# Batch 1's row flags in a graph-attention kernel: from sums on ScalarE, stored and read back, in place of GpSimd's sums and a matmul

## Chip, cores and metric

The kernel runs on one core of a Trainium2 chip. The metric is the device time of one execution in microseconds; lower is better. Times before are the median of three runs; the profile shows one execution.

## The reference

For each of 16 batches there are 512 nodes with 512 features (x), one condition vector (cond), and an integer mask with 11 labels for each pair of nodes. The part that matters here is the row flag: a node whose features sum to zero gets no condition.

```python
row_zero = exp_v.sum(-1) == 0
q_exp = jnp.where(row_zero[..., None], 0.0, q[:, None, :])
vcq = jnp.concatenate([exp_v, q_exp], axis=-1)
self_feat = vcq @ W_self.T + b_self
output = self_feat
for d in range(2):
    # A: the mask (d = 0) or its transpose, first 20 neighbours
    output = output + _gat_attention(self_feat, cond, vb, Wq[d], bq[d], Wk[d], bk[d], Wout[d], bout[d])
return exp_v + jax.nn.relu(output)
```

The attention has 16 heads and attends from every node to the first 20 nodes of its batch. Scores are self_feat times keys plus mask and label bias; their softmax weighs the 20 values.

## The kernel before

Everything is float32, and features lie on the partitions. The order of the instructions on each engine is the order in which the program issues them (a manual schedule, no scheduler); tiles of one tag share a few slots, and an instruction waits until its slot is free.

**Setup.** The keys of all batches are multiplied with the query weights ahead of time, so that a score needs one product with self_feat. The work comes in 22 "key bursts", `keys` (line 541), n = 0 to 21 in the loop at line 600. A burst has 12 to 16 small matmuls (ps_g, line 550) into two pairs of PSUM banks, which ScalarE (line 565) and VectorE (line 567) evict, half each, into a stage tile `st` (tag st, four slots). There are 16 stages, (0,0) to (3,3), four bursts to three stages or nearly so. When a stage is full, SP stores it with three transfers: batch 0's part into `g0` in SBUF (line 570), batch 1's into `g1_d` (line 573) and the others' into `g_d` (line 574, 1120 KB).

The pool of the banks has two slots, so a burst's matmuls wait for the evictions of the burst before. To fill that time a list `other` of side steps (lines 581 to 585) is handed out from burst 4 on (line 610): biases, row flags of batch 0, bias scores, a quarter of a self_feat block, a piece of the values (`values`, line 515), row flags of batch 1, and another self_feat block. Side steps are TensorE work but for the first. The last piece of each value tile is followed by a VectorE copy (line 531) and a store that GpSimd issues (line 533). v00, v01, v10, v11, v20 are those tiles; they share two slots of tag full with the score biases of `full_add`.

Beside the bursts, at fixed n, stand the mask's steps of batch 0: `mask_count` at 6 and 13, `mask_mul` at 7 and 15 (a ScalarE cast, line 210, and a GpSimd product), `mask_add` at 9 with `load_cq(0)`, `full_add` at 18.

**Row flags.** There are two ways in the kernel. For batches 0 and 1, `row_sums` (line 163) adds the four feature blocks of the transposed x with three GpSimd additions, and `row_flags` (line 170) sums over the partitions by a matmul with ones, so that every partition of `nzs[b]` has all 512 flags after a VectorE comparison (line 174). For batches 2 to 15, `load_xn` loads x again with nodes on the partitions, in two halves of 512 KB; `row_sum` (line 148) is a ScalarE ACTIVATE with a running sum, four a batch; `row_mask` (line 154) compares on VectorE and stores 2 KB into `nz_d`; `load_nz` (line 159) reads them back, broadcast to all partitions (256 KB). The flags are read by `self_copy` (line 202), which evicts self_feat.

**Batch loop.** Each of four node tiles (nt) of a batch has 16 score matmuls (ps_s, line 249) and some self_feat matmuls of this or the next batch (ps_sf, line 189); at nt = 2 the values of the batch before are applied (ps_o, line 314). VectorE, ScalarE and GpSimd do the softmax. Batch 1's flags are first read at b = 0, nt = 3. At b = 0, nt = 1, SP issues the loads of batch 1's mask and cq, six stores that clear `bd_d` (`clear_blocks`) and twelve copies that fill it (`blocks`); `load_values` at nt = 2 reads it.

Of the kernel before, what the change touches and what calls it, by code (L numbers as in the profile page):

```python
# [18 lines left out]
def gat_kernel(  # L19
# [24 lines left out]
    C = F // P  # L44
# [45 lines left out]
    def load_xn(b, h):  # L90
        t = xns[b, h] = load.tile([P, 2, F], F32, tag="xn", name=f"xn{b}_{h}")
        nc.sync.dma_start(t, xn[b].rearrange("(p j) f -> p j f", j=4)[:, 2 * h : 2 * h + 2])
# [70 lines left out]
    def row_sums(b):  # L163

        t = rss[b] = load.tile([P, 2, F], F32, tag="xn", name=f"rx{b}")[:, 0]
        nc.gpsimd.tensor_add(t, xs[b][:, 0], xs[b][:, 1])
        for k in range(2, C):
            nc.gpsimd.tensor_add(t, t, xs[b][:, k])
# [176 lines left out]
    with tc.tile_pool(name="setup", bufs=1) as sp:  # L345
# [151 lines left out]
        with tc.tile_pool(name="setup_g", bufs=4) as sg:  # L497
# [83 lines left out]
            other = [(biases, ()), (row_flags, (0,)), (bias_scores, (0,)), (bias_scores, (1,))]  # L581
            other += [(self_step, (0, 0, 0, i, k)) for i in range(2) for k in (0, 2)]
            other += [(values, (t, (d,), k)) for t in range(2) for d in range(2) for k in range(C)]
            other += [(values, (2, (0, 1), k)) for k in range(C)] + [(row_flags, (1,))]
            other += [(self_step, (0, 1, 0, i, k)) for i in range(2) for k in (0, 2)]

            halves = [(fc, hg, d, i) for fc in range(C) for hg in range(C) for d in range(2) for i in range(2)]
# [12 lines left out]
            for n, runs in enumerate(bursts):  # L600
                for i in range(len(rest)):
                    if i < (3 if n == 0 else 1) or any(fc == 0 and (d, hg) == rest[0] for fc, hg, d, _, _ in runs):
                        key_rows(*rest.pop(0))
                keys(runs)
                if rest:
                    for d in range(2):
                        bias_terms(d, n)
                    continue
                first = n if first is None else first
                while done * (len(bursts) - first) < (n + 1 - first) * len(other):  # L610
                    f, args = other[done]
                    f(*args)
                    done += 1
                if n == 6:
                    mask_count(0, 0)
                if n == 7:
                    mask_mul(0, 0)
                if n == 9:
                    mask_add(0, 0)
                    load_cq(0)  # L620
                if n == 11:
                    row_sums(1)
                if n == 13:
                    mask_count(0, 1)
                if n == 15:
                    mask_mul(0, 1)
                if n == 18:
                    full_add(0, 0)

    soft = ctx.enter_context(tc.tile_pool(name="soft", bufs=2))  # L630
    gp = ctx.enter_context(tc.tile_pool(name="gp", bufs=2))
# [3 lines left out]
    with tc.manual_schedule():  # L635
        load_keys(1)

        prev = None
        o = None
        banks = None  # L640
        for b in range(B):
            def ahead(nt):


                if nt < 2:
                    return ((b, nt, 1),)
                return ((b + 1, 0, 0), (b + 1, 1, 0)) if nt == 3 and b + 1 < B else ()

            for nt in range(NT):
                store()  # L650
                if nt == 1:
                    if b + 1 < B:
                        load_adj(b + 1, 0)
                        load_cq(b + 1)
                    if b == 0:
                        clear_blocks(zero)
                        blocks()
                if nt == 2:
                    load_values(b)
                    if b + 1 in rss and b > 0:  # L660
                        load_nz(b + 1)
                    if 0 < b < B - 1:
                        load_keys(b + 1)
                    if b + 2 < B:
                        load_x(b + 2)
                    if b + 1 < B:
                        load_adj(b + 1, 1)
                    if b + 2 < B:
                        load_xn(b + 2, 0)
                        load_xn(b + 2, 1)  # L670

                if prev is not None:
                    normal(*prev)
                ps = ps_s.tile([P, 2, 512], F32, tag="s", name=f"ps_s{b}_{nt}")
                for part in ahead(nt):
                    self_feat(*part)
                if nt == 2 and b > 0:
                    banks = [ps_acc.tile([P, 512], F32, tag="acc", name=f"ps_o{b - 1}_{q}") for q in range(4)]
                    for n in range(2):
                        attend(b - 1, n, [t[:, bass.ts(n, N // 2)] for t in banks])  # L680
                    o = work.tile([P, C, N], F32, tag="o", name=f"o{b - 1}")
                    finish(b - 1, o, (0, 1), banks)
                for g in range(2):
                    scores(b, nt, g, ps)

                if nt == 0 and b > 0:
                    mask_mul(b, 1)
                    mask_count(b, 1)
                if nt == 1:
                    mask_add(b, 1)  # L690
                if nt == 2 and b + 1 < B:
                    mask_mul(b + 1, 0)
                    mask_count(b + 1, 0)
                if nt == 3 and b + 1 < B:
                    mask_add(b + 1, 0)
                last = b == B - 1
                for part in ahead(nt):
                    self_copy(*part)
                if last and nt == NT - 1:
                    s = soft.tile(full, F32, tag="s", name=f"s{b}_{nt}", bufs=3)  # L700
                    weigh_half(b, nt, ps, s, 0)
                    turn(*prev)
                    weigh_half(b, nt, ps, s, 1)
                else:
                    s = weigh(b, nt, ps)
                    expo(s)
                    if prev is not None:
                        turn(*prev)
                if nt < NT - 1:
                    full_add(b, nt + 1)  # L710
                elif b + 1 < B:
                    full_add(b + 1, 0)
                if nt >= 2 and b > 0:
                    residual(b - 1, 2 * nt - 4, o)
                    residual(b - 1, 2 * nt - 3, o)
                if 0 < b < B - 1 and nt < 2:
                    row_sum(b + 1, 2 * nt)
                    row_sum(b + 1, 2 * nt + 1)
                    if nt == 1:
                        row_mask(b + 1)  # L720
                prev = (b, nt, s)
        store()
        b = B - 1
        turn_half(*prev, 0)
        turn_half(*prev, 1)

        o = work.tile([P, C, N], F32, tag="o", name=f"o{b}")
        out_b = out[b].rearrange("(c p) n -> p c n", p=P)
        most = [ps_acc.tile([P, 512], F32, tag="acc", name=f"ps_o{b}_{q}") for q in range(4)]
        pairs = [ps_s.tile([P, 2, 512], F32, tag="s", name=f"ps_o{b}_{q}_2") for q in range(2)]  # L730
        rest = [pairs[q // 2][:, q % 2] for q in range(4)]
        parts = []
        for lo, hi, banks in ((0, NT - 1, most), (NT - 1, NT, rest)):
            width = (hi - lo) * R
            parts.append((slice(2 * lo, 2 * hi), slice(lo * P, hi * P), width, banks))
            for n in range(2):
                attend(b, n, [t[:, bass.ts(n, width)] for t in banks], slice(lo, hi))
        for ts, ns, width, banks in parts:
            for q in range(4):
                c = bass.ds(q // 2 * 2, 2)  # L740

                def of(t):
                    return t[:, c].rearrange("p c (t q n) -> p c t q n", q=2, n=32)[:, :, ts, q % 2]

                nc.vector.tensor_add(  # L745
                    of(o), banks[q][:, : 2 * width].rearrange("p (c t n) -> p c t n", c=2, n=32), of(sfs[b])
                )
            for c in range(C):
                nc.scalar.activation(o[:, c, ns], o[:, c, ns], AF.Relu, bias=bo[:, c : c + 1])  # L749
        ns = parts[0][1]  # L750
        for c in range(3):
            nc.gpsimd.tensor_add(o[:, c, ns], o[:, c, ns], xs[b][:, c, ns])
            nc.sync.dma_start(out_b[:, c, ns], o[:, c, ns])
        ns = parts[1][1]
        nc.vector.tensor_add(o[:, :, ns], o[:, :, ns], xs[b][:, :, ns])
        nc.sync.dma_start(out_b[:, :, ns], o[:, :, ns])
        ns = parts[0][1]
        nc.vector.tensor_add(o[:, 3, ns], o[:, 3, ns], xs[b][:, 3, ns])
        nc.sync.dma_start(out_b[:, 3, ns], o[:, 3, ns])
# [46 lines left out]
```

## Time and profile before

| | us |
|---|---|
| median of 3 runs | 634.22 (633.94 to 636.79) |
| the profiled execution | 634.41 |
| its span, first to last instruction | 632.6 |
| TensorE busy | 618.7 (98%) |
| VectorE busy | 508.4 (80%) |
| GpSimd busy | 337.4 (53%) |
| ScalarE busy | 218.1 (34%) |

The granted TensorE clock is 0.994 of full speed over the span. The chain of work that ended last is followed back from the last instruction: at each step to what released it, or to the instruction before it on its engine. In timelines a row gives start, length, engine, line, operation, tile written and tiles read; a square bracket gives the idle time before it and what ended it. Matmul rows overlap, since they are pipelined. PEld is the loading of weights, which runs beside PE.

### The profile page before, as it was taken

How to read it: one execution, taken by the hardware profiler on the slowest of the kernel's cores; microseconds unless marked ns; L12 is line 12 of the kernel's file. 1: busy time of each engine (PE TensorE's matmuls, PEld its weight loads, DVE VectorE, ACT ScalarE, POOL GpSimd, SP SyncE). 2: the span in 40 equal slices, each digit the busy share in tenths (PEclk: the TensorE clock that was granted, in tenths of full speed). 3: DMA queues.
4: the chain of work that ended last, by engine and by line, in shares of the span. 5: the costliest groups of instructions: out<-in, count | busy, mean ns of one | idle time of the engine just before them, and what ended most of it. 6: DMA issues, size and time to landing. Idle time of an engine off the chain costs nothing.

```text
span 632.6 us, 16385 instructions
## 1 busy us (share of the span) xinstructions
PE 618.7 (98%) x6814; PEld 383.6 (61%) x6814; DVE 508.4 (80%) x815; ACT 218.1 (34%) x480; POOL 337.4 (53%) x258
## 2 busy tenths in 40 slices
PE   8999999999999999999999999999999999999993
PEld 6655459986565656565655656565656565656542
DVE  0566546879888888888888889797988888888886
ACT  1445321233342424242424233343334242424232
POOL 2405331446556464738392938474655646473853
PEclk9999999999999999999999999999999999999997
DMA  8999998628384565738392909292838465663322
GB/s 287 397 382 321 392 371 249 216 88 268 134 237 165 150 253 127 275 90 313 70 333 42 358 19 339 52 292 107 262 141 248 154 207 196 147 256 102 129 68 101
DMA packets 89569, 131.86 MB, mean 208 GB/s; under 512 B 8888, under 2 KB 59608, under 8 KB 87448
## 3 DMA queue, kind: packets, MB, share of 16 engines
q1 hardware_dynamic: 88824, 129.47, 61.7%
q0 software_dynamic: 672, 1.36, 0.8%
q8 instruction: 53, 0.87, 0.6%
q14 instruction: 20, 0.16, 0.1%
HBM read 90.89 MB, written 39.92 MB: 207 GB/s over the span
## 4 chain that ended last, share of the span: by engine, by line
PE 85%; DVE 2%; ACT 1%; issue 0%; DVEq 0%; ACTq 0%
PE ps_s L249 43%; PE ps_sf L189 33%; PE ps_o L314 6%; PE ps_v L523 1%; ACT o L749 0%; PE ps_nz L172 0%; DVE s L287 0%; DVE mx L278 0%; DVE o L745 0%; DVE s L279 0%; PE ps_g(3, 3, 0, 0, 2)0_778 L550 0%; PE ps_g(3, 2, 0, 1, 2)0_752 L550 0%; PE ps_g(3, 1, 1, 0, 2)0_724 L550 0%; PE ps_g(3, 0, 1, 1, 2)0_701 L550 0%; DVE ps_s L276 0%
## 5 line engine op out<-in xcount | busy, mean ns | idle before, releaser
L249 PE MATMUL ps_s<-g,sf 128*64 128x320 f32 x2048 | 287.6, 433 | 0.0
L249 PEld LDWEIGHTS ps_s<-g,sf 128*64 128x64 f32 x2048 | 155.4, 137 | 116.3 <-issue 6.2
L189 PE MATMUL ps_sf<-x,ws_v 128*64 128x256 f32 (+1 forms) x2048 | 222.0, 371 | 0.0
L189 PEld LDWEIGHTS ps_sf<-x,ws_v 128*64 128x64 f32 x2048 | 151.1, 137 | 67.5 <-issue 1.7
L296 POOL TENSOR_TENSOR s<-s,sm 128x640 f32<-128x640 f32 x63 | 80.1, 1271 | 145.5 <-DVE sm L295 134.8
L269 ACT ACTIVATE s<-s 128x640 f32<-128x640 f32 x63 | 46.5, 738 | 220.9 <-DVE s L264 220.9
L239 POOL TENSOR_TENSOR full<-cq,both 128x640 f32<-128x640 f32 x64 | 99.0, 1547 | 27.6 <-ACT both L230 23.5
L211 POOL TENSOR_TENSOR prod<-prod,wb_sb 128x880 f32<-128x880 f32 x32 | 61.3, 1915 | 56.5 <-ACT prod L210 56.5
L260 DVE TENSOR_TENSOR ps_s<-ps_s,full 128x640 f32<-128x640 f32 x63 | 52.3, 831 | 39.4 <-PE ps_s L249 39.4
L336 POOL TENSOR_TENSOR o<-o,x 128x512 f32<-128x512 f32 x60 | 75.5, 1281 | 0.0
L230 ACT COPY both<-add 64x80 f32<-64x80 f32 x128 | 32.8, 256 | 77.4 <-DVE add L225 76.3
L202 DVE SCALAR_TENSOR_TENSOR sf<-nz,qw,ps_sf 128x236 f32<-128x236 f32 (+1 forms) x128 | 52.6, 458 | 3.5 <-PE ps_sf L189 3.5
L333 ACT ACTIVATE o<-o,bo 128x512 f32<-128x512 f32 x60 | 40.0, 714 | 44.3 <-DVE o L327 44.3
L294 DVE TENSOR_REDUCE sm<-s 128x32 f32<-128x640 f32 x63 | 51.6, 818 | 4.4 <-ACT s L269 0.9
L262 DVE TENSOR_REDUCE mx<-ps_s 128x32 f32<-128x640 f32 x63 | 52.0, 825 | 2.2
L264 DVE TENSOR_TENSOR s<-ps_s,mx 128x640 f32<-128x640 f32 x63 | 51.9, 824 | 2.2
L303 DVE STREAM_TRANSPOSE wt<-s 128x640 f32<-128x640 f32 x63 | 52.5, 834 | 0.0
L314 PE MATMUL ps_o<-wt,vd 32*32 32x256 f32 (+2 forms) x2176 | 46.7, 381 | 4.2 <-issue 2.8
L314 PEld LDWEIGHTS ps_o<-wt,vd 32*32 32x32 f32 x2176 | 31.6, 104 | 19.8 <-issue 12.4
L327 DVE TENSOR_TENSOR o<-ps_o,sf 128x512 f32<-128x512 f32 x60 | 36.3, 668 | 0.0
L152 ACT ACTIVATE xn<-xn 128x512 f32<-128x512 f32 x56 | 34.3, 613 | 0.0
L216 DVE TENSOR_REDUCE cond<-adj 128x80 f32<-128x880 int32 x32 | 33.2, 1036 | 0.2 <-DMA adj<-in_adj 0.2
(205 smaller groups left out, 415.7 us busy)
## 6 DMA issues: line engine op xcount, KB each, us to landing
g<-g_d SPq DMA_DIRECT2D x15, 1280.0 KB, 9.0
g_d<-st SPq DMA_DIRECT2D x16, 1120.0 KB, 6.3
x<-in_xT SPq DMA_DIRECT2D x16, 1024.0 KB, 11.0
out_T<-o SPq DMA_DIRECT2D x61, 256.0 KB, 5.0
xn<-in_xn SPq DMA_DIRECT2D x28, 512.0 KB, 8.7
adj<-in_adj SPq DMA_DIRECT2D x32, 440.0 KB, 7.3
vd<-bd_d SPq DMA_DIRECT2D x64, 128.0 KB, 4.1
nz<-nz_d SPq DMA_DIRECT2D x14, 256.0 KB, 4.7
```

The costliest lines, as they stand in the source:

```text
L189: nc.tensor.matmul(held[0][bass.ts(a, R), i * N // 2 : i * N // 2 + hi - lo], ws_v[:, k, bass.ds((2 * f + i) * P + a * R, R)], xs[b][:, k, ...
L202: nc.vector.scalar_tensor_tensor(sfs[b][:, 2 * f + i, lo:hi], nzs[b][:, lo:hi], qw[:, 2 * f + i, b : b + 1], ps[:, i * N // 2 : i * N // 2 ...
L211: nc.gpsimd.tensor_mul(p, p, wb_sb.unsqueeze(1).to_broadcast([P, 2 * S, L]))
L239: nc.gpsimd.tensor_add(f, cqs[b].unsqueeze(1).to_broadcast(shape), adds[b, nt // 2][:, nt % 2].unsqueeze(2).to_broadcast(shape),)
L249: nc.tensor.matmul(ps[bass.ts(a, R), g, : W // 2], sfs[b][:, k, bass.ds(nt * P + g * R, R)], keys[:, k, a], start=(k == 0), stop=(k == C - 1),
L260: nc.vector.tensor_add(pw, pw, fulls.pop((b, nt)).rearrange("p g h m -> p g (h m)"))
L262: nc.vector.tensor_reduce(mx, p4, AX.X, ALU.max)
L264: nc.vector.tensor_sub(s, p4, mx.unsqueeze(3).to_broadcast(full))
L296: nc.gpsimd.tensor_mul(s, s, sm.unsqueeze(3).to_broadcast(full))
L303: nc.vector.transpose(wts[b][:, nt], s.rearrange("p a h m -> p (a h m)"))
L314: nc.tensor.matmul(banks[q][bass.ts(e, DH)].rearrange("p (t n) -> p t n", n=32), vds[b][r, e, i, q // 2 * 2 + n], wt[r, :, bass.ts(j, 32)] ...
L336: nc.gpsimd.tensor_add(o[:, c], o[:, c], xs[b][:, c])
```

## The change

Batch 1 is moved from the first way to the second, in the setup. The side step `row_flags(1)` and the GpSimd additions at n = 11 go. The halves of batch 1's x are loaded at n = 10 and n = 12; ScalarE sums a quarter at each of n = 15 to 18, behind the evictions of that burst; the comparison and the store come at n = 19, and the load of the flags at b = 0, nt = 1, ahead of `clear_blocks`. The list `other` has 32 steps where it had 33, and the loop at line 610 hands them out in the same proportion, so that many stand a little earlier or later.

```diff
-            other += [(values, (2, (0, 1), k)) for k in range(C)] + [(row_flags, (1,))]
+            other += [(values, (2, (0, 1), k)) for k in range(C)]
...
-                if n == 11:
-                    row_sums(1)
+                if n in (10, 12):
+                    load_xn(1, n // 2 - 5)
+                if 15 <= n < 19:
+                    row_sum(1, n - 15)
...
                 if n == 18:
                     full_add(0, 0)
+                if n == 19:
+                    row_mask(1)
...
                     if b == 0:
+                        load_nz(1)
                         clear_blocks(zero)
                         blocks()
```

## The prediction

> **What bounds the kernel.** I read the shares of the chain that ended last, then that chain in order of time over the setup, then TensorE's timeline there, and the busy times by stretch.
>
> ```profile
> PE 85%; DVE 2%; ACT 1%; issue 0%; DVEq 0%; ACTq 0%
> ```
>
> TensorE carries the chain. From 90 us until the last batch's end phase at 611 it never waits: each batch repeats the same 33.35 us (the scores behind ps_o start at 140.22, 173.57, 206.91). So the change can only move the moment at which the batch loop's PE stream begins. That is in the setup, here in the chain in order of time (start, length, what):
>
> ```profile
> 81.25 0.47 PE ps_g(3, 1, 1, 0, 2)0_724 L550 x2
> ...
> 82.27 1.87 PE ps_v L523 x8
> 84.14 0.34 PE ps_g(3, 2, 0, 1, 2)0_752 L550 x2
> ...
> 85.16 1.05 PE ps_nz L172 x2
> 86.22 0.95 PE ps_sf L189 x8
> ...
> 90.41 4.40 PE ps_sf L189 x40
> 94.81 4.45 PE ps_s L249 x32
> ```
>
> The reader sees a key burst (ps_g, 1.02 us), then two side steps of some 0.95 us, then the next burst. ps_nz, the matmul of row_flags(1), is one of these side steps and lies on the chain with 1.05 us. It is a side step that the change removes.
>
> **The matmul goes: 0.94 us.** 33 side steps are spread over bursts 4 to 21, mostly two to a burst; with 32 the spread changes. Counted from lines 581 to 613: single steps stand at bursts 9, 15, 21 before and at 8, 12, 17, 21 after. A single step is not simply 0.95 us shorter, as TensorE's timeline shows (burst 9, 10, 11):
>
> ```profile
> 55.04 0.41 PE L550 MATMUL ps_g(1, 2, 1, 1, 2)0_514<-khT,wq_sb 32*128 32x160 f32 x2
> ...
> 56.06 1.12 PE L523 MATMUL ps_v<-wo_sb,kvT 128*128 128x512 f32 x2
> 57.25 0.54 PE L550 MATMUL ps_g(1, 3, 1, 0, 2)0_545<-khT,wq_sb 32*128 32x320 f32 x2
> 57.60 0.54 PE L550 MATMUL ps_g(1, 3, 1, 0, 2)1_546<-khT,wq_sb 32*128 32x320 f32 x2
> ...
> 60.97 0.41 PE L550 MATMUL ps_g(2, 0, 0, 1, 2)0_569<-khT,wq_sb 32*128 32x160 f32 x2 [0.37 <-ACT st L565]
> ```
>
> Burst 9 with one step takes 57.25-55.04 = 2.21 us, of which 0.24 is waiting for ScalarE's eviction; in burst 10 the second bank starts 0.34 us late, behind VectorE's. So a single costs 0.58 us of waiting. Burst 11 begins after 0.37 us of idle and stretches by 0.10, since line 230's four copies ("both", 1.06 us) stand in ScalarE's queue ahead of burst 10's eviction. Waiting before: two singles x 0.58 + 0.47 = 1.63 us. After: three x 0.58 = 1.74; the 0.47 goes, because burst 9 is then a double and the copies, some 0.4 us sooner, end before PE comes back. Gain: 1.05 - (1.74 - 1.63) = 0.94 us. Bounds: 0.47 if the stall of burst 11 stays; 1.5 if the extra single costs nothing.
>
> **GpSimd's sums go: nothing.** Three additions, 1.28 + 2.62 = 3.9 us at 61.5 to 65.5. GpSimd then waits 1.85 us for the next v tile; nothing waits for rx until the matmul at 85. VectorE's 0.68 us comparison (L174) goes too.
>
> **ScalarE's sums come: nothing on the path.** Four times an ACTIVATE of 613 ns and a reading of 187 ns, by the 56 such pairs of the loop: 0.8 us, or 0.7 where the next instruction overlaps the reading. They stand behind the evictions of bursts 15 to 18, where ScalarE's rows show 2.0 us of idle a burst (1.03 us busy in 2.9). Only burst 15 is tight: eviction, sum 0.7, cast 0.92 (L210), next eviction; 1.03 + 0.8 + 0.92 = 2.75 fits into 2.94. VectorE gets a comparison of 170 ns at burst 19, in the place of the 0.68.
>
> **v20 is evicted one burst later.** Its last matmul moves to burst 19. Its VectorE copy needs v11's slot; v11's store leaves at 79.4 and lands within 3.1 to 6.2 us, so by 85.6, and the copy's turn is near 85.5: up to 0.1 us late, and VectorE has 0.4 us there. full_add(0,1) follows its stores to some 94; its reader (L260) comes at 107.1. Nothing.
>
> **The loads come.** load_xn(1, 0) goes into SP's queue after the stores of stage (1,3), some 63.6, load_xn(1, 1) after those of (2,0), some 67.5: 512 KB each, 0.41 us of issue in the loop, up to 1.36. Queued behind each are the stage stores (L570, L573, L574). The built program gives SP's transfers eight completion counters in turn: none is issued before the one eight ahead has landed. So g0's store of stage (2,2), due at 71.95, now waits for xn1_0, and a store of (2,3), due at 75.8, for xn1_1. And the transfers share a busy stretch (us, PE, PEld, DVE, ACT, POOL, clock, DMA share, GB/s):
>
> ```profile
> 65.00:70.00 5.00, 5.00 (x32) 2.07 (x31) 3.70 (x6) 2.06 (x4) 1.03 (x2) 1.00 1.03 409
> 70.00:75.00 5.00, 4.96 (x38) 2.15 (x38) 3.35 (x7) 2.07 (x5) 0.54 (x1) 1.00 0.98 377
> 75.00:80.00 5.00, 4.98 (x40) 2.72 (x42) 2.66 (x6) 2.53 (x5) 2.49 (x2) 1.00 1.05 408
> 80.00:85.00 5.00, 5.00 (x46) 1.94 (x42) 2.61 (x4) 1.48 (x3) 0.00 (x0) 1.00 0.96 376
> ```
>
> 1.05 MB at 409 GB/s is 2.6 us of all engines. Spare room: against 409 the four slices leave (32 + 1 + 33) x 5 = 0.33 MB; 85 to 90 moves 352 GB/s, 0.28 more. So by 90 us some 0.4 MB, 1.0 us, may still be late, if 409 is the limit, and none if it is higher (single slices reach 430 and more).
>
> A rule speaks against the change here: the Trainium skill, "DMA: Bandwidth & Descriptors", section "Where 436 GB/s comes from", says that transfers between HBM and SBUF are held to about 358 GB/s per core by the HBM. By that rule the stretch has no room at all and the full 1.05 MB, an estimated 2.9 us from that page, would be paid. The rows above, 376 to 409, contradict it.
>
> When does xn land? Bounds: 5.2 us (a 1120 KB store in this stretch) and 9.9 (the slowest xn of the loop, which has x, adj and another xn just ahead). I take 6, nearest to the stores in this stretch: the store of (1,3), issued at 63.03, lands at 68.2, and 0.52 MB more is 1.3 us. Then xn1_0 is there at 69.5, before the 71.95 of the store and the 74 of its sum. Nothing.
>
> **The flags' way home.** nz_d (0.33 us of issue) now stands in SP's queue ahead of g0's store of the last stage, then the nz load (0.34 us, 256 KB) behind cq's:
>
> ```profile
> 89.20 1.31 SPq L574 DMA_DIRECT2D g_d<-st  x1
> ...
> 90.62 0.47 SPq L570 DMA_DIRECT2D g<-st  x1
> 91.14 1.45 SPq L573 DMA_DIRECT2D g_d<-st  x1
> ```
>
> SP has no gap there, so g0's last piece goes 0.4 us later. It lands 3.6 to 5.4 us after issue, so 94.2 to 96.0; the eighth of 16 score matmuls, the first to read it, starts at 94.81 + 7 x 0.28 = 96.8. Slack 0.8 to 2.6, less 0.4, less up to 1.0 of lateness: a stall of 0 to 0.6; I take 0.2. nz's load lands near 106 (2.4 and 4.7 us for the two transfers), its reader (L202) comes at 119. The blocks behind it are 0.4 us later and their vd is needed at 137.5, against a landing near 124. Nothing.
>
> **Sum.** The profiled execution took 634.41 (span 632.6 and 1.8 around it): 634.41 - 0.94 + 0.2 = **633.7**. The median of the runs is 0.19 lower, well within what runs differ.
>
> **Rivals.**
> - The evictions, not PE, set the burst's pace. For: PEld waits 0.8 us for "ACT st" in most bursts; the single costs 0.58. Against: with two steps bursts are back to back. Then the gain is 0.47 or less: 634.0 to 634.4.
> - Slower: xn lands late. Place: SP, at the store of (2,2). If xn1_0 needs over 8.4 us from 63.6, that store waits, and its L574 lands later than 80.1 to 80.9 (73.8 + 6.3 to 7.1); burst 18 needs the slot again at 82.7, in the changed kernel at 81.9. So the case decides from about 9.5 us on, 1.0 beyond. With an issue stretched to 1.4 and 11.0 us, as the 1 MB loads of x take, SP is held until 76: some 3 us on PE, and ScalarE's first sum is late by 1.5 as well, with burst 16's eviction behind it. 634.5 to 638.
> - The lateness of 1.0 to 2.6 us arrives whole at g0's last piece, minus the slack: 634.0 to 636.1.
>
> **Chances.** Forecast 0.53 (632.7 to 633.9, by the bounds 1.5 and 0.5 and the stall); evictions 0.13; late xn 0.18, a third of it beyond 637.6; lateness at g0 0.10; something that I don't see 0.06, half to each side. The likeliest's own range is 632.7 to 633.9; the range over the cases, to leave out no more than 2 in 10, is 632.6 to 636.8. About 0.5% (3.2 us, from 631.2 to 637.6) is what a measurement of this kernel tells from no change: faster 0.03, same 0.88, slower 0.09.
>
> **What would show it.** No ps_nz behind burst 19, single steps after bursts 8, 12 and 17 with 2.2 us each, no idle at burst 11, first scores at 93.9 to 94.1 instead of 94.81, and 33.35 us a batch as before. xn1 loads that land within 7 us. Wrong if scores start later than 94.8, if a ps_g waits for a DMA through st, or if the loop's period changes.

## The result, and the profile after

The changed kernel took 638.94 us (median of 7, 637.89 to 640.58); the kernel before, run beside it, 636.18 (median of 7, 633.94 to 637.15). The ratio is 1.0052 with a 95% interval of 1.0034 to 1.0071: slower by half a per cent. The profiled execution took 638.94 as well, its span is 637.0, and the clock was 0.992 (0.994 before). So 4.4 us of span are to be found between the two profiled executions; the medians differ by 2.8, since the profiled execution of before (634.41) is one of its faster ones.

The shares of the chain that ended last, after:

```profile
PE 89%; DMA 3%; SPq 2%; DVE 2%; ACT 1%; issue 1%; DVEq 0%; ACTq 0%
```

New on it are DMA with 3% and SPq (the issuing of transfers by SyncE) with 2%, which the line of before did not have: for some 30 us the chain now runs through transfers and their issue instead of PE. The chain in order of time (start, length, what) shows where they stand:

```profile
71.67 8.96 DMA g_d<-st
...
80.73 0.71 ACT st L565
...
81.49 0.54 PE ps_g(3, 1, 1, 0, 2)0_726 L550 x2
...
92.06 1.68 SPq L574
...
93.85 0.58 SPq L157
...
94.54 5.21 DMA g<-st
...
99.88 0.45 PE ps_s L249
```

A store of 1120 KB (stage (2,1), issued at 71.67) needs 8.96 us; ScalarE's eviction into the same stage slot waits for it, and burst 18 waits for that eviction. Later, the flags' store (L157) and then g0's last piece stand behind a store whose issue alone takes 1.68 us; the piece lands at 99.75, and the first scores wait for it.

TensorE's timeline of the changed kernel at bursts 9 to 11, and then its three waits (square brackets: idle time before the row, and what ended it):

```profile
54.67 0.54 PE L550 MATMUL ps_g(1, 2, 1, 1, 2)0_513<-khT,wq_sb 32*128 32x160 f32 x4
...
57.95 0.54 PE L550 MATMUL ps_g(1, 3, 1, 0, 2)0_545<-khT,wq_sb 32*128 32x320 f32 x2
...
60.88 0.41 PE L550 MATMUL ps_g(2, 0, 0, 1, 2)0_571<-khT,wq_sb 32*128 32x160 f32 x2
```

```profile
81.49 0.54 PE L550 MATMUL ps_g(3, 1, 1, 0, 2)0_726<-khT,wq_sb 32*128 32x320 f32 x2 [1.19 <-ACT st L565]
...
99.88 2.61 PE L249 MATMUL ps_s<-g,sf 128*64 128x320 f32 x17 [2.45 <-DMA g<-st]
...
142.17 2.69 PE L314 MATMUL ps_o<-wt,vd 32*32 32x256 f32 x122 [0.59 <-issue]
```

Burst 9 is a double now (3.28 us), and burst 11 begins without a wait, as the prediction had it. But three waits are new. The third is the one that no line names: the first six rows of ps_o run, the rest stands for 0.59 us. VectorE's timeline tells why, first of before, then of after:

```profile
126.93 1.07 DVE L216 TENSOR_REDUCE cond<-adj 128x80 f32<-128x880 int32 x1 [0.18 <-DMA adj<-in_adj]
128.03 0.20 DVE L217 TENSOR_SCALAR cond<-cond 128x80 f32<-128x80 f32 x1
```

```profile
131.50 1.07 DVE L216 TENSOR_REDUCE cond<-adj 128x80 f32<-128x880 int32 x1 [1.26 <-DMA adj<-in_adj]
132.60 1.93 DVE L217 TENSOR_SCALAR cond<-cond 128x80 f32<-128x80 f32 x1
...
141.21 0.86 DVE L202 SCALAR_TENSOR_TENSOR sf<-nz,qw,ps_sf 128x256 f32<-128x256 f32 x2
```

VectorE waits 1.26 us for adj(1,1), the second half of batch 1's mask, and its next instruction takes 1.93 us instead of 0.20. GpSimd's timeline, first of before, then of after, shows what ran beside it:

```profile
126.89 1.27 POOL L296 TENSOR_TENSOR s<-s,sm 128x640 f32<-128x640 f32 x1 [4.91 <-DVE sm L295]
```

```profile
132.56 1.92 POOL L211 TENSOR_TENSOR prod<-prod,wb_sb 128x880 f32<-128x880 f32 x1 [0.90 <-ACT prod L210]
```

After, L217 begins 0.04 us behind GpSimd's product with the same mask (L211) and ends 0.05 us behind its end; before, it began 0.13 us ahead of the end of L296 and ended 0.07 us behind it. In all sixteen profiles of this document it ends 0.05 to 0.07 us after the GpSimd instruction that was under way when it began. So 1.1 us more of lateness of adj(1,1) became 2.8 us on VectorE. VectorE is late from there on. Its eviction of self_feat (L202) ends at 142.07, and only then has ps_o its fourth PSUM bank: PE goes on at 142.17. adj(1,1) is the last mask load in SP's queue at b = 0 (line 672), behind `blocks`, `load_values` and x2; it was issued at 122.11 before and at 126.41 after.

To compare executions I divide the span at four marks of PE: the first key burst (24.73 before, 25.04 after), the first scores, the first side matmuls behind them, and the scores behind the first ps_o. What comes ahead of the first key burst differed between all the profiles by up to 2.5 us (23.97 to 26.51), without relation to any edit, and is left out in "in all".

| | key phase | first scores | to the scores behind ps_o | rest | in all |
|---|---|---|---|---|---|
| before | 69.91 | 4.31 | 41.20 | 492.45 | 607.87 |
| after | 70.07 | 6.98 | 42.71 | 492.20 | 611.96 |

The 4.4 us are 0.31 ahead of the first burst, 0.16 in the key phase (0.94 gained, 1.10 lost at burst 18), 2.67 at the first scores, 1.51 on the way to ps_o, less 0.25 in the rest.

The busy times by stretch (us, PE, PEld, DVE, ACT, POOL, clock, DMA share, GB/s), after:

```profile
65.00:70.00 5.00, 4.89 (x31) 2.28 (x34) 4.21 (x7) 2.06 (x4) 0.56 (x1) 1.00 0.98 326
70.00:75.00 5.00, 5.00 (x36) 2.14 (x28) 3.14 (x6) 2.56 (x5) 0.54 (x1) 1.00 1.04 396
75.00:80.00 5.00, 5.00 (x41) 2.18 (x40) 2.41 (x4) 3.12 (x8) 2.50 (x2) 1.00 1.05 419
80.00:85.00 5.00, 3.81 (x36) 1.93 (x38) 2.14 (x3) 2.93 (x7) 1.53 (x1) 1.00 1.02 410
```

In the slice that takes the first load the engines are as busy as before (0.98 against 1.03) and move 326 GB/s instead of 409. The loads take more engine time than their bytes tell, and there was no time left: the share had been 1.0 already. SP shows the same from its side (start, us of issue, line):

```profile
73.31 1.13 SPq L570 DMA_DIRECT2D g<-st  x1
74.49 1.48 SPq L573 DMA_DIRECT2D g_d<-st  x1
76.03 1.18 SPq L574 DMA_DIRECT2D g_d<-st  x1
...
93.85 0.58 SPq L157 DMA_DIRECT2D nz_d<-nz  x1
94.54 1.22 SPq L570 DMA_DIRECT2D g<-st  x1
```

From 73.31 to 97.5 SP issues back to back, and L570, 0.47 to 0.49 us in every stage of before from 63 us on, takes 1.0 to 1.2. In before SP still had 4.4 us of waiting for VectorE's evictions from 63 us on (2.5 of it behind 73.3), which was its reserve. g0's last piece goes at 94.54; before, at 90.62.

### The profile page after: what moved, and what is told of

It reads as the page before. It is cut to its first block, busy times and chain, and to the rows that moved or that the text cites. A ratio compares the mean times of both kernels' runs of the same rounds, so it can differ in the third digit from the quotient of the medians.

```text
span 637.0 us, 16392 instructions
## 1 busy us (share of the span) xinstructions
PE 618.5 (97%) x6812; PEld 376.8 (59%) x6812; DVE 510.1 (80%) x815; ACT 220.4 (35%) x488; POOL 334.1 (52%) x255
## 4 chain that ended last, share of the span: by engine, by line
PE 89%; DMA 3%; SPq 2%; DVE 2%; ACT 1%; issue 1%; DVEq 0%; ACTq 0%
PE ps_s L249 43%; PE ps_sf L189 32%; PE ps_o L314 6%; PE ps_k L472 3%; DMA g_d<-st 1%; DMA ws_q<-in_wsT 1%; PE ps_v L523 1%; DMA g<-st 1%; SPq L573 1%; PE ps_kv L423 1%; ACT st L565 1%; SPq L574 1%; ACT o L754 0%; SPq L570 0%; SPq L386 0%
## 5 line engine op out<-in xcount | busy, mean ns | idle before, releaser
L249 PEld LDWEIGHTS ps_s<-g,sf 128*64 128x64 f32 x2048 | 149.2, 137 | 126.2 <-issue 9.2
L296 POOL TENSOR_TENSOR s<-s,sm 128x640 f32<-128x640 f32 x63 | 80.2, 1273 | 145.4 <-DVE sm L295 145.4
L211 POOL TENSOR_TENSOR prod<-prod,wb_sb 128x880 f32<-128x880 f32 x32 | 61.4, 1919 | 57.2 <-ACT prod L210 57.2
L202 DVE SCALAR_TENSOR_TENSOR sf<-nz,qw,ps_sf 128x236 f32<-128x236 f32 (+1 forms) x128 | 52.6, 458 | 3.5 <-PE ps_sf L189 3.5
L152 ACT ACTIVATE xn<-xn 128x512 f32<-128x512 f32 x60 | 36.8, 614 | 0.0
L216 DVE TENSOR_REDUCE cond<-adj 128x80 f32<-128x880 int32 x32 | 33.1, 1036 | 1.3 <-DMA adj<-in_adj 1.3
```

The costliest lines, as they stand in the source:

```text
L202: nc.vector.scalar_tensor_tensor(sfs[b][:, 2 * f + i, lo:hi], nzs[b][:, lo:hi], qw[:, 2 * f + i, b : b + 1], ps[:, i * N // 2 : i * N // 2 ...
L211: nc.gpsimd.tensor_mul(p, p, wb_sb.unsqueeze(1).to_broadcast([P, 2 * S, L]))
L249: nc.tensor.matmul(ps[bass.ts(a, R), g, : W // 2], sfs[b][:, k, bass.ds(nt * P + g * R, R)], keys[:, k, a], start=(k == 0), stop=(k == C - 1),
L296: nc.gpsimd.tensor_mul(s, s, sm.unsqueeze(3).to_broadcast(full))
```

## Experiments

The main theory: the setup's DMA engines are full, SP issues in order, and 1 MB more makes everything behind it late; the rivals are SP's order (the flags' store), ScalarE's sums, and the new spread of side steps. Each kernel ran in five rounds beside the kernel before. The budgets are of one profiled execution each.

| kernel | median | ratio to before | key phase | first scores | to ps_o's scores | in all |
|---|---|---|---|---|---|---|
| 1 no loads | 636.03 | 1.0016 (1.0003 to 1.0028) | 68.97 | 4.85 | 42.40 | 608.54 |
| 2 only the loads | 637.09 | 1.0030 (1.0014 to 1.0045) | 69.91 | 5.99 | 41.97 | 610.23 |
| 3 flags last | 640.67 | 1.0084 (1.0054 to 1.0113) | 69.76 | 6.33 | 46.25 | 615.17 |
| 4 loads by ScalarE | 638.34 | 1.0057 (1.0038 to 1.0077) | 70.57 | 6.09 | 42.10 | 610.92 |
| 5 adj(1,1) first | 638.20 | 1.0053 (1.0035 to 1.0071) | 70.12 | 6.95 | 41.55 | 610.87 |
| 6 g0 first | 641.54 | 1.0102 (1.0073 to 1.0132) | 70.21 | 4.31 | 43.84 | 610.59 |
| 7 both | 635.21 | 1.0000 (0.9980 to 1.0020) | 70.11 | 4.30 | 41.05 | 607.70 |
| 8 before, both | 634.98 | 1.0001 (0.9988 to 1.0013) | 69.91 | 4.31 | 41.05 | 607.72 |
| 9 loads early | 636.79 | 1.0025 (1.0010 to 1.0041) | 68.97 | 5.78 | 42.87 | 609.81 |
| 10 early, both | 633.39 | 0.9964 (0.9948 to 0.9981) | 68.97 | 4.31 | 41.05 | 606.56 |
| 11 no loads, both | 633.03 | 0.9962 (0.9944 to 0.9981) | 68.98 | 4.30 | 41.05 | 606.67 |
| 12 loads late, both | 633.62 | 0.9965 (0.9946 to 0.9985) | 68.97 | 4.31 | 41.05 | 606.54 |
| 13 no matmul | 634.89 | 0.9995 (0.9980 to 1.0010) | 69.06 | 4.30 | 41.99 | 607.83 |
| 14 flags aside | 635.87 | 1.0008 (0.9989 to 1.0026) | 68.97 | 4.62 | 42.56 | 608.58 |

The median of before beside them was 634.94 (runs 1 to 4), 634.96 (5 to 8), 635.59 (9 to 12) and 635.19 (13 and 14).

**1. Without the loads.**

```diff
-        t = xns[b, j // 2]
-        nc.scalar.activation(t[:, j % 2], t[:, j % 2], AF.Identity, ...)
+        t, i = (xs[1], j) if b == 1 else (xns[b, j // 2], j % 2)
+        nc.scalar.activation(t[:, i], t[:, i], AF.Identity, ...)
...
-                if n in (10, 12):
-                    load_xn(1, n // 2 - 5)
```

> Everything of the change but the two loads of x1 with nodes on the partitions: ScalarE's four sums run in place over the feature blocks of x1 that are in SBUF already (so batch 1's flags no longer tell which of its rows are zero). The flags' store and load stay. Theory 1 (the 1.05 MB of the loads in a stretch where the 16 DMA engines are already full): without them the gain of the matmul is left: 0.5 to 1.5 us faster than the kernel before, no wait of burst 18 for a stage slot, g0's last piece issued by 92 instead of 94.54, no PE wait at the first scores or under 0.6 us. Theory 2 (the flags' store in SP's queue): still 2 us or more slower. Theory 3 (ScalarE's sums or the new spread of side steps): still 2 us or more slower, with bursts 15 to 18 late.

Measured: the key phase is 0.94 us shorter than before, exactly the predicted gain of the matmul, and burst 18 does not wait. So ScalarE's sums and the new spread cost PE nothing (theory 3 falls), and the stage slot's wait is the loads'. Yet the kernel is 0.16% slower than before, not faster. The gain is taken back at the other two places:

```profile
96.37 2.64 PE L249 MATMUL ps_s<-g,sf 128*64 128x320 f32 x17 [0.32 <-DMA g<-st]
```

```profile
127.68 1.07 DVE L216 TENSOR_REDUCE cond<-adj 128x80 f32<-128x880 int32 x1 [0.93 <-DMA adj<-in_adj]
```

PE comes earlier, and the transfers do not. Without the loads 3.4 of the 4.1 us are gone, as theory 1 said, but the 0.5 to 1.5 us of gain that it expected were not there; runs 11, 13 and 14 ask why.

**2. The loads alone.**

```diff
                 if n == 11:
                     row_sums(1)
+                if n in (10, 12):
+                    h = n // 2 - 5
+                    nc.sync.dma_start(wk_sb[1][:, 2 * h : 2 * h + 2],
+                        xn[1].rearrange("(p j) f -> p j f", j=4)[:, 2 * h : 2 * h + 2])
```

> The kernel before, flags by GpSimd and the matmul as they were, plus the same two loads of 512 KB at the same two places of SP's queue, into a weight tile that is no longer read. Theory 1: all of the loss appears without the rest of the change: 3 to 5 us slower than the kernel before (the 4.4 us between the two profiled spans plus the 0.4 to 0.9 us that the matmul's absence gains there), with stage issues stretched to over 1 us and a PE wait of 2 us or more for g0 at the first scores. Theories 2 and 3: the same time as before.

Measured: 2.1 us slower in the medians, 2.36 in the budget, 1.68 of it at the first scores and 0.77 on the way to ps_o. That is less than the 3 to 5 expected: burst 18 does not wait. Counted from the first key burst, PE gets there 1.1 us later than in run 1, with the matmul in place, and the store that held it goes 0.7 us sooner than in the changed kernel; which of the two decides was not tried. The loads do cost with nothing else changed, and their cost depends on how early PE comes to the places where it meets the transfers.

```profile
98.06 2.61 PE L249 MATMUL ps_s<-g,sf 128*64 128x320 f32 x17 [1.46 <-DMA g<-st]
```

**3. The flags' store behind the last stage.**

```diff
-                if n == 19:
+                if n == 21:
                     row_mask(1)
```

> The changed kernel with the comparison and the flags' store moved behind the last burst, so that the store (0.58 us of issue on record, 0.7 with what lies around it) stands behind g0's last piece. Theory 1: g0's last piece goes 0.7 us sooner and the wait at the first scores falls from 2.45 to about 1.8: still 2 to 4 us slower than before. Theory 2: the loss goes, the time is that of before or 1 us less.

Measured: the wait at the first scores shrinks to 1.79 us, as theory 1 said (theory 2 falls: the store's place is worth about 0.7 us there). In all it is slower than the changed kernel, by 3.5 us on the way to ps_o: in this execution the load of adj(1,0) took 10.86 us, SP was held at L129 until 109.5, and VectorE waited 3.92 us for adj(1,1). The single runs spread over 7 us (637.25 to 644.56), so how large this is from run to run stays open; that the second place decides it in this execution is shown.

**4. The loads from ScalarE's queue.**

```diff
-    def load_xn(b, h):
+    def load_xn(b, h, queue=nc.sync):
...
-        nc.sync.dma_start(t, xn[b].rearrange("(p j) f -> p j f", j=4)[:, 2 * h : 2 * h + 2])
+        queue.dma_start(t, xn[b].rearrange("(p j) f -> p j f", j=4)[:, 2 * h : 2 * h + 2])
...
-                    load_xn(1, n // 2 - 5)
+                    load_xn(1, n // 2 - 5, nc.scalar)
```

> The changed kernel with the two loads issued by ScalarE at the same places of the program, so that nothing of them stands in SP's queue and they take none of its completion counters, but the bytes go at the same time. Theory 1 (bytes): the loss stays, 2 to 4 us slower than before, SP's stage issues stretched all the same. Rival (order: an in-order queue with two more transfers in it): half of the loss or more goes, the time is within 1 us of before.

Measured: 3.4 us slower; the loss stays. There was a surprise on ScalarE:

```profile
59.41 4.78 ACTq L92 DMA_DIRECT2D xn<-in_xn  x1
```

The issue of the first load held ScalarE's sequencer for 4.78 us, the eviction of burst 11 came late, and PE stood 1.49 us at burst 12. The second issue took 0.33. This new wait makes the run a less clean test of SP's order: part of the loss is now at burst 12, and the later waits are smaller since PE comes later. Counted from the first key burst, PE leaves the first scores at 76.7 us, against 77.1 as changed and 73.8 without the loads. So most of the lateness comes with the transfers, whichever queue issues them; a small share of SP's order is not excluded.

**5 to 8. SP's order, with and without the change.** Two edits: each alone (runs 5 and 6) and both together (run 7) on the changed kernel, and both on the one before (run 8):

```diff
                         clear_blocks(zero)
+                        load_adj(1, 1)
                         blocks()
...
-                    if b + 1 < B:
+                    if 0 < b < B - 1:
                         load_adj(b + 1, 1)
```

```diff
-            stages = {}
+            stages, late = {}, []
...
-                        nc.sync.dma_start(g_d[C * fc + hg], st[:, 2:])
+                        late.append((C * fc + hg, st))
+                        if (fc, hg) not in ((3, 1), (3, 2)):
+                            for x, t in late:
+                                nc.sync.dma_start(g_d[x], t[:, 2:])
+                            late.clear()
```

> The changed kernel with one load moved in SP's queue: the second half of batch 1's mask, adj(1,1), goes between clear_blocks and blocks instead of behind them, behind load_values and behind x2. Theory A (two places lose: the first scores wait for g0's last piece, and later VectorE waits for adj(1,1), which makes the last weights for ps_o late): the second place falls away, VectorE's wait at L216 and the gap in ps_o go, and 1.2 to 1.8 us of the loss with them; 1.5 to 2.5 us slower than before stay, from g0. Rival B (all of the loss is in the key phase and at g0; VectorE's lateness would be made up before anything waits): no difference from the changed kernel.

Measured: 42.71 becomes 41.55, ps_o runs without a gap, L216 waits for nothing, and the 2.43 us at the first scores stay. (The expectation spoke of late weights; it is the bank that L202 frees, as the timeline above shows.) The place is shown by the profile; in the medians (638.2 against 638.94, from another series) the 1.1 us don't stand out, and 3.2 us slower than before is more than the 2.5 expected.

> The changed kernel with the two 1120 KB stores (L574) of stages (3,1) and (3,2) issued behind g0's piece of (3,3), not ahead of it; every byte still goes before batch 1's loads. Theory A: g0's last piece is issued by 91.5 instead of 94.54, the wait of 2.45 us at the first scores goes (at most 0.5 left), but the later place stays or grows (SP reaches adj(1,1) no sooner): 0.5 to 2.5 us slower than before. Rival B: the whole loss goes but for the 0.4 of burst 18: within 1 us of before. Rival C (the bytes make everything late, whatever their order): no difference from the changed kernel.

Measured: the wait at the first scores is gone (4.31), and g0's last piece went at 91.70. The later place grew: 43.84, with VectorE 2.88 us on adj(1,1). The time is far above what any of the three expected, 641.54, and its profiled execution (638.86) was the fastest of six. Why it is so slow from run to run stays open. In the profiled execution the mask did not come later: counted from the first key burst, adj(1,1) is there 1.4 us sooner than in the changed kernel, but PE leaves the first scores 2.5 us sooner, so the wait is longer. One thing comes with the edit itself: the three stores of 1120 KB now stand together ahead of batch 1's loads, and SP needs 6.82 us to issue one mask load behind them:

```profile
92.86 3.15 SPq L577 DMA_DIRECT2D g_d<-st  x3
96.18 1.08 SPq L111 DMA_DIRECT2D g<-g_d  x1
97.31 6.82 SPq L96 DMA_DIRECT2D adj<-in_adj  x1
```

The same issue takes 7.37 to 7.69 us in runs 7, 8, 10 and 11, where adj(1,1) stands ahead of the blocks and nothing waits for it.

> Both edits of the two runs above on the changed kernel. Theory A: both places are covered; what stays is the stage slot's wait at burst 18 (1.2 us in the changed kernel's profile) against the matmul's 0.9: within 1 us of before.

> Both edits on the kernel before, without the change. Theory A: the kernel before has next to no wait at the two places in its profiled execution, so it gains 0 to 1 us, mostly in those executions that ran near 636.8; the changed kernel with both edits is within 1 us of it. Rival: if the change costs something else, the distance to the run before this one stays at 2 us or more.

Measured: with both edits the change costs nothing (ratio 1.0000), and the kernel before with both gains nothing (1.0001). Both as theory A said. Covering the two places takes 4.3 us off the changed kernel's budget, all of its loss; what is left of the change is 0.94 gained and 1.14 lost at bursts 18 and 19 (waits of 0.44 and 0.69), which the key phase of 70.11 shows. No single edit did it: covering the later place left the earlier one as it was (run 5), and covering the earlier one made the later one longer (run 6).

**9 to 12. Where the bytes go.**

```diff
-                if n in (10, 12):
-                    load_xn(1, n // 2 - 5)
+                if n in (4, 5):
+                    load_xn(1, n - 4)
```

> The changed kernel with the two loads at n = 4 and 5 in place of 10 and 12, where the DMA engines have gaps (share 0.77 of 45 to 50 us and 273 GB/s in the kernel before). Theory A (a backlog that forms from 65 us on and never drains): the gaps take 0.5 to 1 MB, so the kernel comes close to the one without loads: 0.5 to 2 us slower than before, from the first key burst to the end 608.5 to 610 (608.5 without the loads, 612.0 as changed). Rival (the bytes cost the same wherever they go, since the queue never drains after 49 us): 3 to 4 us slower, 611 or more.

Measured: 1.2 us slower than before, 609.81 in all, as theory A said. The gaps at 43 to 53 us took the loads. First before, then the early loads:

```profile
43.00:48.00 5.00, 4.94 (x53) 2.74 (x54) 3.60 (x13) 2.59 (x6) 1.80 (x3) 1.00 0.76 300
48.00:53.00 5.00, 5.00 (x64) 3.08 (x58) 4.10 (x8) 2.48 (x6) 3.95 (x7) 1.00 0.91 242
```

```profile
43.00:48.00 5.00, 5.00 (x57) 2.89 (x59) 3.60 (x13) 2.79 (x7) 2.24 (x4) 1.00 1.02 401
48.00:53.00 5.00, 5.00 (x59) 3.10 (x56) 3.80 (x9) 2.20 (x6) 3.96 (x6) 1.00 1.00 309
```

Burst 18 waits no more and the key phase has its 0.94. The rest of the loss, 1.25 us of wait at g0 and 1.43 at adj(1,1), stays.

> The early loads with both edits of SP's order (g0's last piece ahead of two stores, adj(1,1) ahead of the blocks). Theory A: the matmul's 0.9 us is no longer taken back: 606.5 to 607.3 from the first key burst to the end, against 607.9 before, and a median 0.3 to 1.2 us below the kernel before. Rival: 607.7 or more.

> Both edits on the kernel without the loads (its sums run over x1's feature blocks, so batch 1's flags tell nothing): what the change could bring at most. Theory A: no wait at the three places, 606.7 to 607.0 from the first key burst to the end, 0.9 to 1.1 us less than the kernel before. Rival (the gain is taken back by a fourth place): 607.6 or more.

> The loads behind the key phase: the two loads go where batch 1's keys were loaded (behind the last stage), the four sums stand behind batch 0's first exponentials, comparison, store and load of the flags follow at nt = 1; the keys' load goes behind clear_blocks, and both edits of SP's order are in. Theory A: the key phase has no wait, the flags are there before 119: 606.7 to 607.5 from the first key burst to the end, 0.3 to 1.1 us less than before. Rival: the flags' way (load, sums, store, load) ends after 119 and holds VectorE's first eviction with them: 609 or more.

Run 12 moves more than the loads: they go where `load_keys(1)` stood, that goes behind `clear_blocks`, the four sums behind batch 0's first exponentials, and comparison, flags' store and load, adj(1,1) and `blocks` follow in this order at nt = 1.

Measured: all three keep the gain, 606.5 to 606.7 in all, and run 0.35 to 0.38% below the kernel before. Run 10 beats both kernels: 633.39 against 635.59 beside it, ratio 0.9964 (0.9948 to 0.9981). It is the change as it was made, the loads six to seven bursts earlier, and two edits of SP's order. Its loads cost nothing that run 11, without them, would show.

```profile
94.31 4.48 PE L249 MATMUL ps_s<-g,sf 128*64 128x320 f32 x32
...
136.99 2.76 PE L314 MATMUL ps_o<-wt,vd 32*32 32x256 f32 x128
```

Neither row has a wait in front of it.

**13 and 14. Why nothing was left without the loads.**

```diff
-        ps = ps_acc.tile([P, 512], F32, tag="acc", name=f"ps_nz{b}")
-        nc.tensor.matmul(ps[:, :N], ones, rss[b], start=True, stop=True)
+        if b == 0:
+            ps = ps_acc.tile([P, 512], F32, tag="acc", name=f"ps_nz{b}")
+            nc.tensor.matmul(ps[:, :N], ones, rss[b], start=True, stop=True)
+        else:
+            ps = rss[b]
...
-            other += [(values, (2, (0, 1), k)) for k in range(C)] + [(row_flags, (1,))]
+            other += [(values, (2, (0, 1), k)) for k in range(C)]
...
+                if n == 19:
+                    row_flags(1)
```

> The kernel before without the matmul ps_nz and with nothing added: the comparison reads GpSimd's sums as they are, not summed over the partitions (so batch 1's flags tell nothing), at n = 19. Theory D (no slack: in the kernel before g0's last piece lands some 0.7 us ahead of its reader and VectorE already waits 0.18 us for adj(1,1), so a PE stream that is 0.94 sooner runs into both): from the first key burst to the first scores 0.9 less, from there to the end 0.3 to 0.9 more, in all 607.0 to 607.6 against 607.9. Rival (in the run without the loads the flags' store and load took the gain): the whole 0.94 stays, 606.9 or less.

Measured: the same time as before (0.9995, 0.9980 to 1.0010). The key phase is 0.85 us shorter, and 0.79 comes back on the way to ps_o, where VectorE (here lines 219 and 205, for 216 and 202) waits for the same load:

```profile
126.01 1.07 DVE L219 TENSOR_REDUCE cond<-adj 128x80 f32<-128x880 int32 x1 [1.02 <-DMA adj<-in_adj]
...
135.73 0.86 DVE L205 SCALAR_TENSOR_TENSOR sf<-nz,qw,ps_sf 128x256 f32<-128x256 f32 x2
```

```profile
135.72 0.63 PE L317 MATMUL ps_o<-wt,vd 32*32 32x256 f32 x6
136.69 2.70 PE L317 MATMUL ps_o<-wt,vd 32*32 32x256 f32 x122 [0.35 <-issue]
```

L205 ends at 136.59, PE goes on at 136.69. So a matmul taken away, with nothing put in its place, gains nothing here. Of theory D the half on adj(1,1) holds, with a little more loss than it gave (607.83 against 607.0 to 607.6); the half on g0 does not, since the first scores take 4.30 with no wait.

```diff
-                    row_mask(1)
+                    row_mask(1, nc.gpsimd)
...
-                        load_nz(1)
+                        load_nz(1, nc.scalar)
```

> The kernel without the loads (608.5 from the first key burst to the end), with the flags' store issued by GpSimd and their load by ScalarE instead of SP, so that nothing of the change is left in SP's queue. Theory D: g0's last piece goes 0.7 us sooner than there and adj(1,1) 0.6 to 1.2, the result is that of the run without the matmul, 607.0 to 607.7. Rival (the bytes of the flags' load, not its place, cost): 608.2 or more.

Measured: 608.58, as without the edit. Nothing was gained by taking the flags out of SP's queue. It is 0.75 us above run 13, and that is open: SP reaches `load_keys(1)` 0.78 us later than there, ahead of the flags' load, so this load's bytes are not the reason. One execution each, and medians whose intervals overlap, don't settle it.

## Why the prediction was wrong

**The matmul's 0.94 us: right.** Single steps of 2.26 us (predicted 2.2), no idle at burst 11, and a key phase of 68.97 instead of 69.91 wherever the transfers are out of the way (runs 1, 9 to 12).

**GpSimd's sums, ScalarE's sums, v20: right,** nothing on the path (key phases of runs 1 and 11).

**The loads: wrong, and this is the step that failed.** The text said: "So by 90 us some 0.4 MB, 1.0 us, may still be late, if 409 is the limit, and none if it is higher", and took 6 us for a landing. It counted spare room in bytes, as the distance of each slice's GB/s from 409. But slices of fewer GB/s were not emptier: those of 376 and 377 had shares of 0.96 and 0.98. By the share there was next to no room, and none was found: from 65 to 85 us the changed kernel moved 7.76 MB where before had moved 7.85, with 1.05 MB more to move. The same two loads took a median of 7.6 us in run 2 (the loop's own loads, on which the bound of 9.9 rests, took 7.4 at the least), the store at 71.67 took 8.96, and SP, which had 4.4 us of waiting to spare, lost it. So the term "g0's last piece goes 0.4 us later" was mis-sized: counted from the first key burst, it went 3.6 us later. The 2.9 us that the prediction estimated from the Trainium skill ("DMA: Bandwidth & Descriptors", section "Where 436 GB/s comes from") and rejected came nearer to what was paid than the 0.2 in the sum. That is no point for its reason: the limit of 358 GB/s does not hold here, where run 2 moved 424 GB/s from 78 to 83.

**The stall at g0's last piece: the right place, the wrong size.** Taken as 0.2, bounded by 0.6; measured 2.67. The third rival ("arrives whole") named it and put it at up to 2.6. A slot's wait at burst 18, in the second rival, came too: 1.1. The slot was another, though: the rival named the store of stage (2,2), and the one that was late is that of (2,1), through an eviction of burst 17. The two were given as rivals of each other and came together.

**"Nothing" for what stands behind in SP's queue: wrong.** The prediction moved the blocks by 0.4 us and checked vd, which had 13 us. It did not look at the next load behind it, adj(1,1), whose reader already waited 0.18 us. This cost 1.51.

**The premise.** "From 90 us until the last batch's end phase at 611 it never waits ... So the change can only move the moment at which the batch loop's PE stream begins." The first sentence is right and the second does not follow from it. An engine without a wait can have waits right beside it: at 126.93 VectorE had already waited for the mask, so slack was zero (run 13), and a PE stream that starts 0.94 us sooner needs its transfers 0.94 us sooner. Even with loads that cost nothing, the forecast's gain would not have come with SP's order as it stood (runs 1 and 13).

In sum: 638.94 less 633.7 is 5.2 us; 1.1 at burst 18, 2.5 at the first scores (2.67 less 0.2) and 1.5 on the way to ps_o make 5.1 of it.

## What to carry to other kernels

Read spare DMA room from the engines' share of busy time and from the waits left in the issuing queue, not from GB/s: at a share of 1.0 the next transfer is paid by everything behind it, here as far as 75 us on. Before a gain on the bound engine is booked, list the transfers that it consumes downstream and the idle time in front of each reader; a reader with 0.2 us of wait has no slack, even if the bound engine never stops. When a queue is late, covering one place alone leaves an earlier one as it is or lengthens a later one: go through all of them together, and move what can go early into a stretch where the share is below one.

## What the runs showed of the hardware

- The issue of a transfer is not a constant. SP's 80 KB piece took 1.0 to 1.2 us of issue in the changed kernel instead of 0.47, and up to 1.93 (run 1), a mask load 6.82 (run 6), and the same 512 KB load 4.78 us on ScalarE against 0.33 (run 4): there it held the evictions. The share alone does not set it: it was near 1.0 in before too, where the piece took 0.47.
- The same 512 KB loads lower the bytes that a full stretch moves: 327 GB/s from 63 to 68 us in run 2 at a share of 1.01, against 393 at 1.01 before.
- VectorE's comparison of 128x80 (L217, batch 1's second) took 0.20 us before, 0.51 where adj(1,1) came first, and 1.92 to 1.93 wherever adj(1,1) was late by 0.5 us or more. In each case it ended 0.05 to 0.07 us after the GpSimd instruction that was under way at its start: L296 (128x640) in the first two, the product L211 (128x880) in the third. That it waits for the end of that instruction is read from these times, not tried.
